# A graph attention layer: picking rows out of SBUF from the first step to the last, parts of x made in the start-up, and a reordered end

## The chip, the cores and the metric

The kernel runs on one core of one Trainium2 chip. The metric is the device time of one execution in microseconds; before the change it is 1790.13 us, the median of 3 runs (1790.07 to 1792.62).

## The reference, cut to what matters

There are 6250 nodes with 64 features and 206250 edges, sorted by destination. Queries, keys and values are linear in x; every edge weighs them with a projection of its own attributes.

```python
Qh = (x @ Wq.T + bq).reshape(n, H, D)          # H = 4, D = 16
Kh = (x @ Wk.T + bk).reshape(n, H, D)
Vh = (x @ Wv.T + bv).reshape(n, H, D)
Ee = (edge_attr @ We.T + be).reshape(-1, H, D)
score = (Kh[src] * Qh[dst] * (1.0 / np.sqrt(D)) * Ee).sum(-1)
score = jnp.exp(jnp.clip(score, -5.0, 5.0))
msg = Vh[src] * score[..., None]
wV = jax.ops.segment_sum(msg, dst, num_segments=n)
out = layernorm(x + wV)
```

## The kernel before, in words

**Tiles, groups, steps.** 128 edges make a tile (1612 tiles), 8 tiles a group (202 groups; the last has 4 tiles). A step is two groups (steps 0 to 96), and in the end one group (steps 97 to 104): NS is 105. In a tile an edge is a partition; a step's k and v lie in one of five buffers kvs (KVB), step s in number s % 5.

**The start-up.** Keys and values of all nodes go into the table kv_tab in DRAM (L320 to L323), queries, split into three bf16 parts, into q_tab (L350 to L360). For the first four groups (steps 0 and 1) the rows of x are gathered instead of k and v (L230, xs), turned on TensorE (L375, tp), copied (L378, xe), and multiplied with the weights (L380 adds the bias, L382), and the result is copied to kvs (L384). There are eight such halves, one after another. Then GpSimd gathers k and v for steps 2 and 3 (L402, one indirect DMA a tile), and the main branch begins.

**A step.** `products` (L602, L603) multiplies k by the queries and the edge projection, `scores` (L609 to L612) sums, clips and exponentiates, `message` (L619, L622) multiplies v by the score. The message is split into three bf16 parts by `minus` (L630 takes away what L632 has copied, twice), and `sums` of the next step (L638) adds the edges of each destination with one-hot matrices (L585, of), `add` (L652) puts that into accumulators. The queries of the next step come from a window of the query table by one-hot rows (`spread` L555, `onehot_rows` L572 and L577, `queries` L595). `edges` (L388, L391) projects the edge attributes. PSUM tiles of queries and edge projections have one buffer each, so a step's queries come after the last remainder of the step before.

**Where k and v of a tile come from.** Most tiles are gathered by GpSimd (`gather`, called with s + 4 in step s, behind the message). For every sixth step one tile is fetched row by row from SP's queue (`fetch_rows`, `rows_fetched`). And for steps 6 to 96 the last two tiles are *picked*: x is kept in SBUF as three bf16 parts (parts, 50 blocks of 125 rows), and a one-hot matrix of the source (hot, 25 blocks a half, made on DVE from the turned sources, L481) picks the rows by 50 matrix products (L491) for each tile. `sources` (L466, far, on ACT) and `sources_turned` (L471) give the sources, `picked` (L498, xp) adds the three parts, `picked_turned` (L505, L507) turns them, `picked_kv` (L513 to L516) makes k and v. Step s picks for step s + 2. Constants: M0 = 4 is the first picking step, LAST = 94 the last.

**The parts.** They are made in steps 0 to 3 (`table_parts`, `table_parts_rest`): x comes in again on SP's queue (raw, L448), ACT and DVE split it (L450 to L458). A memset clears the tile first (L427).

**Order.** The schedule is written out by hand: each engine executes its instructions in the order of the program, and each waits for its operands by semaphores. The order of a step is the loop that the change edits (L708 to L786).

**The end.** Blocks of 128 destinations are closed as they fill up (`close`, L668), their statistics taken (`spreads`, L677 and L678), and normed in batches (`roots` L681 and L682, `scales` L685, `norm` L688, with a DMA out, L691). The last block is added from PSUM by `last_add` (L696, L697).

Of the kernel before, what the change touches and what calls it, by code (L numbers as in the profile page):

```python
# [14 lines left out]
P = 128  # L15
N = 6250
# [21 lines left out]
CB = 10  # L38
KVB = 5
XG = 4  # L40
TB = 8
M0 = 4
PAD = N
SPARE = N + 1
TABLES = 4
# [12 lines left out]
def groups_of(s):  # L58
    return range(STEPS[s][0], STEPS[s][0] + STEPS[s][1])
# [1 line left out]

LAST = NS - 8 - 3


def picks_in(s):
    return M0 <= s <= LAST

# [33 lines left out]
def tile_gnn(ctx: ExitStack, tc: tile.TileContext, x, xT, wT, bias, beT, weT, eT, src, dst, dst_rows,  # L103
# [50 lines left out]
    be_p = consts.tile([3, G, C], BF16, name="be_p")  # L154
    wkv = consts.tile([P, 2, 2 * C], F32, name="wkv")
    bkv_p = consts.tile([3, G // 2, 2 * C], BF16, name="bkv_p")
    minus_b = consts.tile([P, P], BF16, name="minus_b")

    acc = consts.tile([P, RING, 4, C], F32, name="acc")
# [24 lines left out]
    with tc.tile_pool(name="nodes", bufs=1) as nodes, \  # L184
# [182 lines left out]
            fetch_queries(g)  # L367


        for g in range(XG):  # L370
            for h in range(2):
                tp = npsum.tile([P, 2, P], F32, name="tp", bufs=2)
                for u in range(2):
                    j = 4 * h + 2 * u
                    nc.tensor.transpose(tp[:, u, :],  # L375
                                        XS[g][:, j:j + 2, :].rearrange("p j c -> p (j c)"), ident)
                xe = nodes.tile([P, 2, P], F32, name="xe", bufs=2)
                nc.scalar.activation(xe, tp, AF.Copy)  # L378
                pv = npsum.tile([P, 4, 2 * C], F32, name="pv", bufs=2)
                nc.tensor.matmul(pv, ones_b, bkv_p, start=True, stop=False, skip_group_check=True)  # L380
                for u in range(2):
                    nc.tensor.matmul(pv[:, 2 * u:2 * u + 2, :], xe[:, u, :], wkv, start=False,  # L382
                                     stop=u == 1, skip_group_check=True)
                nc.scalar.activation(kv_of(g)[:, 4 * h:4 * h + 4, :], pv, AF.Copy)  # L384

    def edge_values(pe, et, n):

# [6 lines left out]
    def keys(t0):  # L394

        n = min(KEYS, T - t0)
        nc.vector.tensor_scalar(key_i[:, :n], dst_i[:, t0:t0 + n], P - 1, None, op0=OP.bitwise_and)
        nc.vector.tensor_copy(key[:, t0:t0 + n], key_i[:, :n, None].to_broadcast([P, n, 2]))

    def gather_kv(g, j):  # L400
        t = g * G + j
        nc.gpsimd.indirect_dma_start(  # L402
            out=kv_of(g)[:, j, :], out_offset=None, in_=kv_tab[:, :],
            in_offset=bass.IndirectOffsetOnAxis(ap=src_i[:, t:t + 1], axis=0))

    for g in range(XG, 2 * KVB - 2):
        for j in range(G):
            gather_kv(g, j)

    rv = nc.values_load(n_wide[0:1, 0:1], min_val=0, max_val=NR2 * 4)  # L410

    with tc.If(rv == 0) as branch:

        with tc.tile_pool(name="work", bufs=2) as work, \
# [11 lines left out]
            parts = accp.tile([P, NB, 3, C], BF16, name="parts")  # L426
            nc.vector.memset(parts, 0.0)  # L427
            NX = N // NB
            x_v = x.rearrange("(p b) c -> p b c", p=NX)
            n_picks = LAST - M0 + 1  # L430
            src_f = accp.tile([P, n_picks, 2], F32, name="src_f")
            t0 = (M0 + 3) * 2 * G - 2
            for i in range(2):
                nc.vector.tensor_copy(src_f[:, :, i],
                                      src_i[:, t0 + i:t0 + i + 2 * G * (n_picks - 1) + 1:2 * G])
            pick = fixed.tile([P, 4 * P], F32, name="pick")
            rows3 = pick[:, :6 * C].rearrange("p (k i c) -> p k i c", k=2, i=3)
            HOT, FAR, X = {}, {}, {}
# [2 lines left out]

                return ap.rearrange("p (a b) -> p a b", b=2)

            def table_parts(b):

                n = min(TB, NB - b)
                raw = work.tile([P, TB, C], F32, name="raw", bufs=1)
                nc.sync.dma_start(raw[:NX, :n], x_v[:, b:b + n, :])  # L448
                rest = pick[:NX, :n * C].rearrange("p (b c) -> p b c", b=n)
                nc.scalar.activation(rest, raw[:NX, :n], AF.Copy)  # L450
                nc.scalar.activation(parts[:NX, b:b + n, 0], raw[:NX, :n], AF.Copy)
                return rest

            def table_parts_rest(b, rest):
                n = min(TB, NB - b)
                nc.vector.tensor_sub(rest, rest, parts[:NX, b:b + n, 0])
                nc.scalar.activation(parts[:NX, b:b + n, 1], rest, AF.Copy)
                nc.vector.tensor_sub(parts[:NX, b:b + n, 2], rest, parts[:NX, b:b + n, 1])  # L458

            def sources(s, i):  # L460

                if picks_in(s):
                    FAR[s, i] = work.tile([P, P], BF16, name="far")
                    nc.scalar.activation(FAR[s, i], row50, AF.Identity,  # L466
                                         bias=src_f[:, s - M0, i:i + 1], scale=-1.0)
# [42 lines left out]
            def picked_kv(s):  # L510
                if picks_in(s):
                    xe, kv = X.pop(s)
                    nc.tensor.matmul(kv, ones_b, bkv_p[:, :2], start=True, stop=False,  # L513
                                     skip_group_check=True)
                    nc.tensor.matmul(kv, xe, wkv, start=False, stop=True, skip_group_check=True)  # L515
                    nc.scalar.activation(kvs[(s + 2) % KVB][:, 2 * G - 2:, :], kv, AF.Copy)  # L516

            def gather(s):
                for g in groups_of(s):
                    for j in range(tiles_of(g)):  # L520
                        if is_rowed(s) and (g - STEPS[s][0]) * G + j == COLUMN:
                            continue
                        if not picks_in(s - 2) or g == STEPS[s][0] or j < G - 2:
                            gather_kv(g, j)

            RS, RK = {}, {}
# [157 lines left out]
            def scales(lo, hi):  # L684
                nc.vector.reciprocal(rstd[:, lo:hi], rstd[:, lo:hi])  # L685
# [12 lines left out]
                                               op0=OP.mult, op1=OP.add)  # L698

            closed, scaled, normed = 0, 0, 0  # L700
            keys(0)
            for k, g in enumerate(groups_of(0)):
                onehot_rows(g, spread(g))
# [1 line left out]
                edges(0, k)  # L705
            queries(0)
            onehot_edges(0)
            for s in range(NS):  # L708
                more = s + 1 < NS
                for g in groups_of(s):  # L710
# [9 lines left out]
                    onehot_rows_rest(nexts[0])  # L720
                if s:
                    sums(s - 1)
                sources_turned(s, 1)
                sources_turned(s + 1, 0)
                if nexts[1:]:
                    onehot_rows(nexts[1], spread(nexts[1]))
                making = [b for b in range(s * 2 * TB, (s + 1) * 2 * TB, TB) if b < NB]
                if making:
                    rest = table_parts(making[0])
                prod = products(s)  # L730
                picked(s - 1)
                if more:
                    edges(s + 1, 0)
                picks(s, 0, 0)
# [5 lines left out]
                msg = message(s, score)  # L740
                if s + KVB - 1 < NS:
                    gather(s + KVB - 1)
                picked_turned(s - 1)
                if nexts[1:]:
                    edges(s + 1, 1)
                minus(s, msg, 0)
                hots(s, 1, 0)
                picks(s, 0, 1)
                minus(s, msg, 1)
                picked_kv(s - 1)  # L750
                if not more:

                    close(B - 2)
                    spreads(B - 2)
                hots(s, 1, 1)
                picks(s, 1, 0)
                sources(s + 1, 1)
                sources(s + 2, 0)
                if s + 1 < NS:
                    rows_fetched(s + 1)  # L760
                if more:
# [1 line left out]
                        keys(nexts[0] * G)  # L763
                    onehot_edges(s + 1)
                    queries(s + 1)
                picks(s, 1, 1)
                hots(s + 1, 0, 0)
                hots(s + 1, 0, 1)
                if more:
# [13 lines left out]
                for i, b in enumerate(making):  # L783
                    if i:
                        rest = table_parts(b)
                    table_parts_rest(b, rest)  # L786
# [12 lines left out]
    with branch.Else():  # L799

        sums = [dram.tile([NR, C], F32, name=f"sums{i}") for i in range(TABLES)]
        with tc.tile_pool(name="gconsts", bufs=1) as gc, \
                tc.tile_pool(name="gloads", bufs=3) as loads, \
                tc.tile_pool(name="ggath", bufs=4) as gath, \
# [28 lines left out]
            def gather(g, j):  # L833
                if j == 0:
                    Q[g] = gath.tile([P, G, C], F32, name="gq")
                t = g * G + j
                if g >= 2 * KVB - 2:
# [125 lines left out]
```

## Time and profile before

| what | number |
|---|---|
| the profiled execution | 1789.88 us, span 1788.0 us |
| mean granted TensorE clock | 0.951 |
| PE | 1638.5 us busy, 92% of the span, 15751 instructions |
| DVE | 1481.6 us, 83% |
| ACT | 914.0 us, 51% |
| POOL | 1337.4 us, 75% |
| gathers of k and v (L402) | 1383, mean 944 ns |
| rows fetched on SP's queue (rk) | 1920 |
| picks (L491) | 9100 matrix products, 828.3 us |
| hots (L481) | 364, mean 1813 ns |

The page gives for each engine its busy time, then groups of equal instructions with their number, mean time and the idle time in front of them. POOL is GpSimd; SP issues most DMAs; PEld is TensorE's loading of weights, which overlaps its products. A timeline line has start and length in us, engine, line of the program, operation, output and inputs with their shapes, how many, and in brackets how long the engine had been idle and what ended that.

### The profile page before, as it was taken

To read this page: it belongs to the slowest core of one execution; us is meant where nothing else is said; L and a number is where in the kernel's file an instruction comes from. 1 tells how busy PE (TensorE), PEld (TensorE's weight loads), DVE (VectorE), ACT (ScalarE), POOL (GpSimd) and SP (SyncE) were. 2 spreads that over 40 slices of the span, in tenths; PEclk is the share of its full clock that TensorE was granted. 3 is DMA by queue.
4 is the path that set the end of the run, shared out by engine and by line. 5 is a ranking of instruction groups with operands and counts; after the bars stand their busy time and mean duration, and the time that the engine had idled before them with its cause. 6 is when DMAs were issued, how large, how long until landed. Compare 5 with 4: busy or idle time off the path is not lost.

```text
span 1788.0 us, 44286 instructions
## 1 busy us (share of the span) xinstructions
PE 1638.5 (92%) x15751; PEld 1369.6 (77%) x15751; DVE 1481.6 (83%) x1695; ACT 914.0 (51%) x1328; POOL 1337.4 (75%) x1427
## 2 busy tenths in 40 slices
PE   8978999999999998999999899999989998999864
PEld 8647888888888787787887778777877887787632
DVE  6459999999998898888889888888988888898654
ACT  3465555555554464454455445455544554455443
POOL 7777777777777777777777777777777777777774
PEclk9968999999999999999999999999999999999855
DMA  7443333333333333332333333323332333333331
GB/s 221 132 121 84 90 93 94 93 94 92 93 81 94 93 86 89 92 94 80 93 93 81 93 81 93 92 81 99 87 93 80 94 93 81 93 90 81 91 80 44
DMA packets 109970, 166.71 MB, mean 93 GB/s; under 512 B 69196, under 2 KB 71452, under 8 KB 109626
## 3 DMA queue, kind: packets, MB, share of 16 engines
q0 software_dynamic: 45280, 91.78, 19.4%
q1 hardware_dynamic: 64074, 71.01, 14.1%
q8 instruction: 125, 2.05, 0.5%
q10 hardware_dynamic: 384, 1.00, 0.3%
q14 instruction: 107, 0.88, 0.2%
HBM read 156.33 MB, written 7.33 MB: 92 GB/s over the span
## 4 chain that ended last, share of the span: by engine, by line
PE 38%; POOL 29%; issue 14%; DVE 13%; DMA 4%; ACT 3%; DVEq 0%; SPq 0%; POOLq 0%; ACTq 0%
POOL kv L402 29%; PE pick L491 18%; PE pe L391 5%; DVE hot L481 5%; DMA kv<-kv_tab,src_i 3%; PE pq L630 2%; PE small L638 2%; DVE prod L603 2%; DVE prod L602 2%; PE pb L555 2%; PE pe L388 2%; PE pb L515 1%; PE pq L595 1%; DVE pq L619 1%; PE ps L350 1%
## 5 line engine op out<-in xcount | busy, mean ns | idle before, releaser
L402 POOL DMA_INDIRECT kv<-kv_tab,src_i x1383 | 1305.3, 944 | 421.7 <-issue 399.8
L491 PE MATMUL pick<-parts,hot 128*128 128x192 bf16 x9100 | 828.3, 249 | 0.0
L491 PEld LDWEIGHTS <-hot 128*128 128x128 bf16 x9100 | 771.7, 99 | 38.1
L481 DVE TENSOR_TENSOR hot<-small,block 128x3200 bf16<-128x3200 bf16 x364 | 645.3, 1813 | 0.4 <-PE pick L491 0.4
L572 ACT ACTIVATE to<-pb,minus_row 126x1024 bf16<-126x1024 f32 x202 | 222.7, 1102 | 371.0 <-PE pb L555 367.2
L632 ACT ACTIVATE msg<-pq 128x1024 bf16<-128x1024 f32 (+2 forms) x210 | 207.6, 989 | 222.3 <-PE pq L630 222.3
L391 PEld LDWEIGHTS pe<-we_sb,et 128*128 128x128 f32 x1612 | 209.7, 203 | 133.4 <-issue 95.3
L602 DVE TENSOR_TENSOR prod<-kv,pq 128x1024 f32<-128x1024 f32 (+2 forms) x105 | 123.5, 1176 | 169.3 <-DMA kv<-kv_tab,src_i 52.0
L391 PE MATMUL pe<-we_sb,et 128*128 128x128 f32 x1612 | 250.3, 302 | 0.0
L577 ACT ACTIVATE to<-to,one_p 126x1024 bf16<-126x1024 bf16 x202 | 230.6, 1142 | 3.5
L638 PEld LDWEIGHTS <-of 128*128 128x128 bf16 x1612 | 145.3, 102 | 31.1 <-issue 7.9
L638 PE MATMUL small<-msg,of 128*128 128x192 bf16 x1612 | 161.9, 257 | 0.5 <-ACT msg L632 0.5
L388 PE MATMUL pe<-be_p,ones_b 3*128 3x512 bf16 x202 | 79.7, 395 | 86.3 <-DVE prod L603 86.1
L630 PE MATMUL pq<-msg,minus_b 128*128 128x512 bf16 x404 | 128.0, 396 | 33.1 <-ACT msg L622 19.5
L622 ACT ACTIVATE msg<-pq 128x1024 bf16<-128x1024 f32 (+2 forms) x105 | 103.8, 989 | 96.8 <-DVE pq L619 96.8
L609 DVE TENSOR_REDUCE small<-prod 128x64 f32<-128x1024 f32 (+2 forms) x105 | 123.6, 1177 | 14.5 <-PE small L471 8.8
L555 PE MATMUL pb<-key_rows,ident_b 112*128 112x512 bf16 x403 | 127.9, 400 | 2.8 <-ACT to L572 2.8
L603 DVE TENSOR_TENSOR prod<-prod,pe 128x1024 f32<-128x1024 f32 (+2 forms) x105 | 123.6, 1177 | 3.6
L619 DVE TENSOR_TENSOR pq<-kv,small 128x1024 f32<-128x1024 f32 (+2 forms) x105 | 123.4, 1175 | 1.4 <-ACT small L612 1.4
L585 DVE TENSOR_TENSOR of<-small,key 128x2048 bf16<-128x2048 bf16 (+2 forms) x105 | 122.9, 1171 | 0.3
L595 PEld LDWEIGHTS <-to 126*128 126x128 bf16 x1612 | 63.5, 101 | 25.3 <-issue 25.1
L612 ACT ACTIVATE small<-small 128x64 f32<-128x64 f32 (+2 forms) x105 | 21.7, 207 | 111.1 <-DVE small L611 109.2
(129 smaller groups left out, 996.4 us busy)
## 6 DMA issues: line engine op xcount, KB each, us to landing
et<-in_eT SPq DMA_DIRECT2D x100, 512.0 KB
rk<-kv_tab SPq DMA_DIRECT2D x1920, 0.5 KB
kv<-kv_tab,src_i POOLq DMA_INDIRECT x1383
qw<-q_tab SPq DMA_DIRECT2D x202, 15.8 KB
kv_tab<-kv_sb SPq DMA_DIRECT2D x5, 640.0 KB
q_tab<-q SPq DMA_DIRECT2D x5, 480.0 KB
acc<-in_x SPq DMA_DIRECT2D x48, 32.0 KB
out<-y SPq DMA_DIRECT2D x48, 32.0 KB
```

The lines of the kernel that those rows point to most:

```text
L391: nc.tensor.matmul(pe[:, 2 * u:2 * u + 2, :], et[:, u, :], we_sb, start=False, stop=u == n // 2 - 1, skip_group_check=True)
L402: nc.gpsimd.indirect_dma_start(out=kv_of(g)[:, j, :], out_offset=None, in_=kv_tab[:, :], in_offset=bass.IndirectOffsetOnAxis(ap=src_i[:, t ...
L481: nc.vector.tensor_tensor(HOT[s, i, h].rearrange("p b (a c) -> p b a c", c=2), pairs(from_b[i])[:, None].to_broadcast(shape), block2[:, bl ...
L491: nc.tensor.matmul(rows3[:, i], hot[:, k, :], parts[:, b], start=b == 0, stop=b == NB - 1)
L555: nc.tensor.matmul(pb[:, b:b + 4, :], ident_b[:NR2, g // 2:g // 2 + 1].to_broadcast([NR2, P]), key_rows[:, g % 2, b * P:(b + 4) * P], star ...
L572: nc.scalar.activation(TO[g][:, :n, :], pb[:3 * W, :n, :], AF.Square, bias=minus_row3[:3 * W])
L577: nc.scalar.activation(TO[g][:, :n, :], TO[g][:, :n, :], AF.Relu, bias=one_p[:3 * W], scale=-1.0)
L602: nc.vector.tensor_mul(prod[:, :n, :], kvs[s % KVB][:, :n, :C], PQ[s][:, :n, :])
L603: nc.vector.tensor_mul(prod[:, :n, :], prod[:, :n, :], PE[s][:, :n, :])
L630: nc.tensor.matmul(msg[:, lo:hi, :], minus_b, M3[s][:, lo:hi, i, :], start=False, stop=True, skip_group_check=True)
L632: nc.scalar.activation(M3[s][:, :n, i + 1, :], msg[:, :n, :], AF.Copy)
L638: nc.tensor.matmul(PA[s], OH[s][:, j, :], M3[s][:, j], start=j == 0, stop=j == n - 1)
```

## The change

It does four things.

- Picking runs from step 0 to the last steps. Steps 0 to 96 pick two tiles for step s + 2; after that three pairs are picked over two single steps each (97 and 98 for step 100, 99 and 100 for 102, 101 and 102 for 104). `second_of` says whose second tile a step works on. 18 gathers less are issued: two in each of steps 2, 3, 4, 5, 97, 98, 100, 102 and 104. The program has 1365 gathers of k and v in this branch, 10050 picks and 402 hots.
- The parts of x are made in the start-up, from xT_sb, which is in SBUF there anyway: four blocks of 128 rows at a time are turned on TensorE into a ps tile, split by ACT and DVE. Thirteen such blocks stand between the k and v of the first groups, two to a half, and the next half's rows are turned ahead of them. The memset and the loads of raw go; parts moves into the pool of constants.
- Before step 0 the first sources, and the hots of its first tile, are made.
- At the end `last_add`, `spreads` and `roots` of the last block go ahead of `scales` and `norm` of the block before it.

The other branch (not executed with these inputs) loses one buffer and gathers what the first loop no longer does.

```diff
-TB = 8
-M0 = 4
+TB = 4
-LAST = NS - 8 - 3
+LAST = NS - 8 - 1
+PAIRS = [*range(LAST + 1), *range(LAST + 1, NS - 3, 2)]
+TARGET = {p: p + (2 if p <= LAST else 3) for p in PAIRS}
-def picks_in(s):
-    return M0 <= s <= LAST
+def picks_in(p):
+    return p in PAIRS
+def second_of(s):
+    return s if s <= LAST else s - 1 if s - 1 in PAIRS else None
+def is_picked(g, j):
+    s = max(s for s in range(NS) if STEPS[s][0] <= g)
+    return s in TARGET.values() and g == groups_of(s)[-1] and j >= tiles_of(g) - 2
...
+        def x_turned(g, h):
+            tp = npsum.tile([P, 2, P], F32, name="tp", bufs=2)
+            for u in range(2):
+                j = 4 * h + 2 * u
+                nc.tensor.transpose(tp[:, u, :], XS[g][:, j:j + 2, :].rearrange("p j c -> p (j c)"),
+                                    ident)
+            xe = nodes.tile([P, 2, P], F32, name="xe", bufs=2)
+            nc.scalar.activation(xe, tp, AF.Copy)
+            return xe
...
+        def parts_of_x(b):
+            n = min(TB, NB - b)
+            px = npsum.tile([P, 2, 2 * C], F32, name="ps").rearrange("p i (j c) -> p (i j) c", j=2)
+            px = px[:, :n]
+            for u in range(n):
+                nc.tensor.transpose(px[:, u, :], xT_sb[:C, (b + u) * P:(b + u + 1) * P],
+                                    ident[:C, :C])
+            nc.scalar.activation(parts[:, b:b + n, 0], px, AF.Copy)
+            nc.vector.tensor_sub(px, px, parts[:, b:b + n, 0])
+            halves.append((px, b, n))
+        def rest_of_x():
+            px, b, n = halves.pop(0)
+            nc.scalar.activation(parts[:, b:b + n, 1], px, AF.Copy)
+            nc.vector.tensor_sub(parts[:, b:b + n, 2], px, parts[:, b:b + n, 1])
+        xe = x_turned(*order[0])
+        for i, gh in enumerate(order):
+            following = x_turned(*order[i + 1]) if i + 1 < len(order) else None
+            for b in blocks[2 * i:2 * i + 2]:
+                parts_of_x(b)
+            first_kv(*gh, xe)
+            xe = following
+            while halves:
+                rest_of_x()
...
     for g in range(XG, 2 * KVB - 2):
         for j in range(G):
-            gather_kv(g, j)
+            if not is_picked(g, j):
+                gather_kv(g, j)
...
+            sources(0, 0)
+            sources_turned(0, 0)
             keys(0)
...
             onehot_edges(0)
+            sources(0, 1)
+            sources(1, 0)
+            for h in range(2):
+                hots(0, 0, h)
             for s in range(NS):
...
-                sources_turned(s, 1)
+                sources_turned(second_of(s), 1)
                 sources_turned(s + 1, 0)
...
-                making = [b for b in range(s * 2 * TB, (s + 1) * 2 * TB, TB) if b < NB]
-                if making:
-                    rest = table_parts(making[0])
                 prod = products(s)
-                picked(s - 1)
+                picked(second_of(s - 1))
...
-                picked_turned(s - 1)
+                picked_turned(second_of(s - 1))
...
-                hots(s, 1, 0)
+                hots(second_of(s), 1, 0)
                 picks(s, 0, 1)
                 minus(s, msg, 1)
-                picked_kv(s - 1)
+                picked_kv(second_of(s - 1))
...
-                hots(s, 1, 1)
-                picks(s, 1, 0)
-                sources(s + 1, 1)
+                hots(second_of(s), 1, 1)
+                picks(second_of(s), 1, 0)
+                sources(second_of(s + 1), 1)
                 sources(s + 2, 0)
...
-                picks(s, 1, 1)
+                picks(second_of(s), 1, 1)
                 hots(s + 1, 0, 0)
                 hots(s + 1, 0, 1)
...
             close(B - 1)
-            scales(B - 2, B - 1)
-            norm(B - 2)
             last_add(NS - 1)
             spreads(B - 1)
             roots(B - 1, B)
+            scales(B - 2, B - 1)
+            norm(B - 2)
             scales(B - 1, B)
             norm(B - 1)
```

More of the change, by code (lines that the diff above doesn't have):

```diff
@@ L156, in tile_gnn @@
     bkv_p = consts.tile([3, G // 2, 2 * C], BF16, name="bkv_p")
+    parts = consts.tile([P, NB, 3, C], BF16, name="parts")
     minus_b = consts.tile([P, P], BF16, name="minus_b")
@@ L367, in tile_gnn @@
             fetch_queries(g)
[L370 to L384, printed above, removed]
+        def x_turned(g, h):
[7 more added lines that the diff above has]
+            return xe
@@ new lines, in first_kv @@
+        def first_kv(g, h, xe):
+            pv = npsum.tile([P, 4, 2 * C], F32, name="pv", bufs=2)
+            nc.tensor.matmul(pv, ones_b, bkv_p, start=True, stop=False, skip_group_check=True)
+            for u in range(2):
+                nc.tensor.matmul(pv[:, 2 * u:2 * u + 2, :], xe[:, u, :], wkv, start=False,
+                                 stop=u == 1, skip_group_check=True)
+            nc.scalar.activation(kv_of(g)[:, 4 * h:4 * h + 4, :], pv, AF.Copy)
+        halves = []
+        def parts_of_x(b):
[8 more added lines that the diff above has]
+            halves.append((px, b, n))
@@ new lines, in rest_of_x @@
+        def rest_of_x():
+            px, b, n = halves.pop(0)
+            nc.scalar.activation(parts[:, b:b + n, 1], px, AF.Copy)
+            nc.vector.tensor_sub(parts[:, b:b + n, 2], px, parts[:, b:b + n, 1])
+        order = [(g, h) for g in range(XG) for h in range(2)]
+        blocks = list(range(0, NB, TB))
+        xe = x_turned(*order[0])
[7 more added lines that the diff above has]
+                rest_of_x()
@@ L424, in tile_gnn @@
             nc.tensor.transpose(col, row_b[:, 0:1].to_broadcast([P, P]), ident_b)
[L426 to L432, printed above, removed]
-            for i in range(2):
-                nc.vector.tensor_copy(src_f[:, :, i],
-                                      src_i[:, t0 + i:t0 + i + 2 * G * (n_picks - 1) + 1:2 * G])
+            src_f = accp.tile([P, PAIRS[-1] + 1, 2], F32, name="src_f")
+            full = NS - 8 - 2
+            for i in range(2):
+                t0 = 3 * 2 * G - 2 + i
+                nc.vector.tensor_copy(src_f[:, :full, i],
+                                      src_i[:, t0:t0 + 2 * G * (full - 1) + 1:2 * G])
+            for p in PAIRS[full:]:
+                t0 = STEPS[TARGET[p]][0] * G + tiles_in(TARGET[p]) - 2
+                nc.vector.tensor_copy(src_f[:, p], src_i[:, t0:t0 + 2])
             pick = fixed.tile([P, 4 * P], F32, name="pick")
@@ L442, in pairs @@
                 return ap.rearrange("p (a b) -> p a b", b=2)
[L444 to L458, printed above, removed]
             def sources(s, i):
@@ L466, in sources @@
                     nc.scalar.activation(FAR[s, i], row50, AF.Identity,
-                                         bias=src_f[:, s - M0, i:i + 1], scale=-1.0)
+                                         bias=src_f[:, s, i:i + 1], scale=-1.0)
             def sources_turned(s, i):
@@ L515, in picked_kv @@
                     nc.tensor.matmul(kv, xe, wkv, start=False, stop=True, skip_group_check=True)
-                    nc.scalar.activation(kvs[(s + 2) % KVB][:, 2 * G - 2:, :], kv, AF.Copy)
+                    n = tiles_in(TARGET[s])
+                    nc.scalar.activation(kvs[TARGET[s] % KVB][:, n - 2:n, :], kv, AF.Copy)
             def gather(s):
@@ L522, in gather @@
                             continue
-                        if not picks_in(s - 2) or g == STEPS[s][0] or j < G - 2:
+                        if not is_picked(g, j):
                             gather_kv(g, j)
@@ L782, in tile_gnn @@
                             normed += 1
[L783 to L786, printed above, removed]
             assert normed == B - 2
@@ L803, in tile_gnn @@
                 tc.tile_pool(name="gloads", bufs=3) as loads, \
[L804 removed]
+                tc.tile_pool(name="ggath", bufs=3) as gath, \
                 tc.tile_pool(name="gwork", bufs=2) as work, \
@@ L836, in gather @@
                 t = g * G + j
-                if g >= 2 * KVB - 2:
+                if g >= 2 * KVB - 2 or is_picked(g, j):
                     gather_kv(g, j)
```

## The prediction, made before the changed kernel ran

> **What bounds the kernel now.** I read the costliest groups first, then the waits, the windows, and the timeline at both ends.
>
> ```profile
> L402 POOL DMA_INDIRECT kv<-kv_tab,src_i x1383 | 1305.3, 944 | 421.7 <-issue 399.8
> ...
> L481 DVE TENSOR_TENSOR hot<-small,block 128x3200 bf16<-128x3200 bf16 x364 | 645.3, 1813 | 0.4 <-PE pick L491 0.4
> ```
>
> ```profile
> POOL kv L402 <- issue: 399.8, 1311, 0.3
> ```
>
> In the second (who waited for whom: total, times, longest) the reader is to see the last number. Busy and idle of the gathers make 1727.0 us for 1383, a pitch of 1.2487 us, and no gap before one is over 0.3 us. So POOL never waits for work: it runs from the first gather (43.04 in the timeline) to 1769.79. What comes after that is a tail of 18 us.
>
> ```profile
> 180.00:225.00 45.00, 45.00 (x474) 38.84 (x475) 42.67 (x42) 23.66 (x36) 34.02 (x37) 1.00 0.33 89
> ...
> 1710.00:1755.00 45.00, 30.64 (x152) 18.71 (x150) 24.22 (x56) 23.71 (x33) 34.08 (x36) 0.58 0.32 84
> ```
>
> The columns are the stretch, its length, busy time of PE, PEld, DVE, ACT, POOL, then granted clock, DMA share, GB/s. In the first row PE and DVE are full: a step with picks needs 15.65 us of PE, while its 14 gathers need 17.5. POOL starts some 40 us ahead, loses 1.6 us a step and is the pace from about 390 us on; the last eight steps (97 to 104, one group each, no picks) are something else, the third view:
>
> ```profile
> 1746.68 0.69 DVE L602 TENSOR_TENSOR prod<-kv,pq 128x512 f32<-128x512 f32 x1 [2.59 <-PE pq L595]
> ...
> 1753.85 0.94 POOL L402 DMA_INDIRECT kv<-kv_tab,src_i  x1 [0.30 <-issue]
> 1754.08 0.58 PE L595 MATMUL pq<-qw,to 126*128 126x64 bf16 x8 [0.69 <-ACT msg L632]
> ...
> 1756.58 0.69 DVE L602 TENSOR_TENSOR prod<-kv,pq 128x512 f32<-128x512 f32 x1 [4.27 <-PE small L638]
> ...
> 1758.58 2.08 PE L391 MATMUL pe<-we_sb,et 128*128 128x128 f32 x8
> ```
>
> Step 101 starts its product at 1746.68; its queries (L595) for step 102 end at 1754.66, 8.0 us later, and the product of 102 then waits for its last gather (issue ends 1754.79, 1.8 us to land). So a single step has an 8 to 8.6 us chain of its own (product, score, message, two remainders, queries) beside 10 us of POOL. The product starts of steps 96 to 104 are 1696.65, 1708.91, 1718.43, 1728.84, 1738.05, 1746.68, 1756.58, 1766.65, 1774.05: only 102 and 103 clearly wait for gathers. From 96 to 104 it is 77.4 us, of which the gathers could give back about 3.5.
>
> **Removed gathers.** 18 of 1383 go: 8 in steps 2 to 5, 10 in steps 97, 98, 100, 102, 104. At 1.2487 that is 10.0 us ahead of step 96, and 12.5 behind it, the latter of use only if POOL still sets the pace there.
>
> **The start.** POOL's own start (43.04) isn't touched. Its first wait is for a buffer: step 5 is gathered into step 0's buffer and needs the message of step 0 (L619).
>
> ```profile
> 76.37 0.60 ACT L384 ACTIVATE kv<-pv 128x512 f32<-128x512 f32 x1 [2.16 <-PE pv L382]
> ...
> 77.08 1.06 PE L555 MATMUL pb<-key_rows,ident_b 112*128 112x512 bf16 x2
> ...
> 84.97 1.22 DVE L602 TENSOR_TENSOR prod<-kv,pq 128x1024 f32<-128x1024 f32 x1 [1.24 <-PE pq L595]
> ...
> 90.33 1.23 DVE L619 TENSOR_TENSOR pq<-kv,small 128x1024 f32<-128x1024 f32 x1 [1.36 <-ACT small L612]
> ```
>
> That message ends at 91.56 now; the gathers of step 5 begin at 102.9, 11 us of slack. After: POOL is there 6 gathers sooner for steps 2 to 4 (28+14 gathers, 43.04 + 42 x 1.2487 = 95.5). The message comes later. Fifty 64-row transposes of x stand in PE's queue among the first k and v, where PE is already full (8.00 of 8.00 in each of the windows 60 to 68 and 68 to 76). A transpose isn't in the trace in this shape; nearest is L350 (same weight load, 17.99 us for 84, 0.214 each): 10.7 us. Bounds: 0.12, the f32 weight load at full clock (L391, 0.97 for 8), 6 us; 0.43, the spacing of L375's two weight loads, 21 us. I take 10.7, less 0.7 for the wait for xe that goes (4.1 in all, mostly under L380): 10. Their 26 copies on ACT (0.38 each) and 26 subtractions on DVE (0.42) lie beside PE, with both nearly idle there; without that cover some 10 us each. Then the first turning of sources comes before L555 in PE's queue, behind src_f (DVE, 0.5 after small's first write) and far (ACT, 0.4): 1.6 us. Gone from the first steps are the memset (4.06, under the wait for L595 until 84.97: worth 0), the raw loads on SP, and L450 and L451 ahead of the exponential of step 0 (0.9). The 3.6 us of hots ahead of product 0 fill the memset's place. Message 0 then ends at 91.56 + 10 + 1.6 - 0.9 + 0.3 = 102.6, and **POOL idles 7.1 us** at its first gather of step 5 (bounds 3 and 18). The gathers of step 6 come up 14 pitches later, at 120, and their buffer (step 1's) is free at about 118: no second stall. Nothing else stands behind the waiting gather than the later gathers, and nobody needs them yet: the price is paid from about step 30 on, where POOL sets the pace. Product 96 so moves by -10.0 + 7.1 = **-2.9 us**. Steps 0 to 3 took 16 us each on the slow chain of the parts; with picks they take 15.65.
>
> **The end.** Here hots (1.81 us each, the L481 row) enter steps 96 to 102: 4, 2, 4, 0, 4, 0, 2. The diff also does one thing twice: `second_of(97)` is 96, as it is for 96, so step 97 repeats two hots and 50 picks of pair 96. In DVE's order hots stand behind the message and ahead of the next product. A single step's DVE rows in the timeline: first product 0.72 to the next start, second 0.69, score 0.69, clip 0.2, 0.5 until the exponential is back, two adds 0.66, message 0.66: it ends 4.0 after the product's start if the sums of the step before are out of the way, 4.6 with xp (0.55). Then a pair of hots 3.54, of 0.68, norms 0.76.
> - Step 96: the full step's DVE chain, 14.55 (product 1645.36 to the end of hots 1659.91), with a shorter of (-0.5) and a close (1.1): 15.1.
> - 97: PE's queue (full clock, it was just busy): edges from 1.45 to 2.95 (L388 and L391, 1.5), 25 picks (2.06) to 5.0, the turn of xp to 5.3, first remainder, 25 picks to 7.6, second remainder 8.0, k and v of the pair 8.9, 25 picks 10.95, queries 11.5: 11.6 (DVE needs 9).
> - 98: on DVE products 1.4, xp after PE's last 25 picks 2.65, then the wait for the sums queued behind those picks 3.5, message 6.05, hots 9.6, of 10.3, hots 13.8, close 14.9, root and three norms: 16.3.
> - 100: message 4.0, hots 7.6, of 8.2, hots 11.8, norms: 12.6. 102: 9.0.
> - 99 and 101: 50 picks lie between the message and the queries: 10.7 (an exp table load included) and 9.5 at full clock. 103 with xp and k and v of the pair: 8.2.
>
> Here a rule counts. The Trainium skill (TensorE: Matmul & The Clock Gate, "What's actually happening") says the array runs at half clock after about 3.4 us of idleness and doubles after as much sustained work. The rows agree: L391's eight take 2.08 at the end, where the clock is 0.58, 1.16 at 1648, and 25 picks after a wait 3.74 (at 1666) against 2.23. By the rule alone picks would warm the tail and pay for some of themselves; but 98 and 100 leave PE idle for over 3 us, so 99 and 101 begin cold: 12.1 each. I take the middle, 11.4 and 10.8. Sum: 15.1 + 11.6 + 16.3 + 11.4 + 12.6 + 10.8 + 9.0 + 8.2 = 95.0, against 77.4: **+17.6** (all warm +15.6, all cold +20.4). A clock or a hidden wait can't take it below what DVE alone has to do, 74 us in these steps by the same rows (some 42 now, 29 of hots, 3 of xp), so the lower end is -3, if nothing waited for anything; I keep to the chain. The gathers of 97 to 104 are through some 20 us earlier than used, so their 12.5 us are worth nothing.
>
> **The last norms.** In DVE's order the last sum t (L696, 1781.12) stands behind the root, scale and norm of the block before; its sums are out of PE at 1780.0. With these moved behind it, t starts about 0.8 sooner, and the two norms end close together: **-0.7** (bounds 0 and -1). The pool of 3 buffers instead of 4 lies in the branch that isn't run: 0.
>
> **Sum.** Profiled execution: 1789.88, span 1788.0, 1.9 around it. -2.9 + 17.6 - 0.7 = +14.0: span 1802.0, time 1803.9; the median of the runs is 0.25 above the profiled one: **1804**.
>
> **Rivals.**
> 1. POOL still paces the tail (faster). The hots would fit in DVE's idle time: it is busy 24.2 of 45 us in 1710 to 1755. Then all 22.5 us count, less 7.1 and 0.7 more: 1774. It decides if the picking steps average under 8.6 us. Against it: DVE's queue is in order, 29 us of added hots are bunched, four in one step, and idle DVE time is mostly waiting on the chain.
> 2. No stall at step 5 (transposes at 0.12, buffer free by 96): 1790.1 - 10.0 + 17.6 - 0.7 = 1797, slower still.
> 3. Start and tail worse: transposes at 0.43 (stall 18) and a cold tail: 1818.
> 4. A wash: no stall, warm tail, and a repeated pair that hides (3 us): 1792.
>
> **Chances.** Main case 0.68, own range 1798 to 1811 (the stall from 3, tail +15.6 to +20.4 and one us either way). Rival 1: 0.09; 2: 0.09; 3: 0.09; 4: 0.05. Main, 2 and 3 are slower. About 0.2% (3.6 us) is what a measurement can tell from no change: faster 0.09, same 0.05, slower 0.86. Range for 8 in 10: 1792 to 1814 (rivals 1 and 3 stay outside).
>
> **What would show it.** Right: one gap of some 7 us on POOL near 95 and none after; product 96 about 3 us earlier; POOL's last gather near 1754, with 20 us of slack; DVE full in steps 98 and 100, those 16 and 13 us long; 10050 picks. Wrong: POOL's gap absent (2), product waits on gathers in 97 to 103 and steps of 8 to 10 us (1), transposes of x at over 0.3 us each (3).

## The result, and the profile after

The changed kernel takes 1799.1 us, the median of 5 runs (1797.59 to 1802.61), against 1790.13 before (5 runs, 1790.07 to 1792.62): a ratio of 1.0049, with a 95% interval of 1.0034 to 1.0064. It is half a per cent slower. The profiled execution took 1800.04 us with a span of 1798.2, so 10.2 us of span more than before. Eleven of the twelve experiments below ran on three chips on which the kernel before itself takes 3066 to 3100 us, and one (the end's order) on a chip on which it takes 1792; so the total times of the eleven tell nothing about the 1799, and from their traces only stretches are read that the disturbance leaves alone.

The page's groups, with the same columns as before:

```profile
L448 POOL DMA_INDIRECT kv<-kv_tab,src_i x1365 | 1288.7, 944 | 417.9 <-issue 395.7
L521 PE MATMUL pick<-parts,hot 128*128 128x192 bf16 x10050 | 914.7, 249 | 0.0
...
L511 DVE TENSOR_TENSOR hot<-small,block 128x3200 bf16<-128x3200 bf16 x402 | 712.5, 1813 | 0.1
```

18 gathers are gone, and 38 hots came (67.2 us of DVE). Who waited for whom, for the gathers:

```profile
POOL kv L448 <- issue: 395.7, 1298, 0.3
...
POOL kv L448 <- DVE pq L650: 2.4, 2, 2.1
```

The second line is new: POOL waited twice for a message (L650), once for 2.1 us. The timeline at that place, with the message of step 0 and the first gather of step 5:

```profile
94.70 0.94 POOL L448 DMA_INDIRECT kv<-kv_tab,src_i  x1 [0.30 <-issue]
96.23 1.23 DVE L650 TENSOR_TENSOR pq<-kv,small 128x1024 f32<-128x1024 f32 x1 [0.27 <-ACT small L643]
...
97.73 0.94 POOL L448 DMA_INDIRECT kv<-kv_tab,src_i  x1 [2.08 <-DVE pq L650]
```

2.08 where 0.30 is usual: a stall of 1.8 us. No other gap ahead of a gather is over 0.35. The windows of the prediction:

```profile
180.00:225.00 45.00, 44.77 (x470) 38.37 (x471) 41.88 (x46) 24.76 (x36) 33.95 (x36) 1.00 0.35 93
1710.00:1755.00 45.00, 36.35 (x347) 30.42 (x346) 34.16 (x49) 19.85 (x34) 30.18 (x32) 0.92 0.28 75
```

The middle is as it was. In the tail DVE does 34.16 us of work where it did 24.22, and TensorE's granted clock is 0.92 where it was 0.58. Steps 96 and 97, from product to product, before:

```profile
1696.65:1708.91 12.26, 5.46 (x31) 3.07 (x30) 7.28 (x11) 4.42 (x5) 9.21 (x11) 0.64 0.21 54
1708.91:1718.43 9.52, 6.26 (x38) 4.03 (x37) 4.21 (x8) 4.23 (x6) 7.39 (x8) 0.68 0.42 115
```

and after:

```profile
1689.09:1704.75 15.66, 14.39 (x156) 12.70 (x154) 14.68 (x17) 6.27 (x9) 11.93 (x13) 1.00 0.21 56
1704.75:1716.57 11.82, 11.82 (x130) 10.53 (x128) 8.13 (x12) 5.41 (x10) 8.85 (x10) 1.00 0.36 98
```

Step 96 is now filled by DVE (14.68 of 15.66 us), step 97 by PE (all of 11.82). What DVE does in step 98, product to product:

```profile
1716.57 0.69 DVE L633 TENSOR_TENSOR prod<-kv,pq 128x512 f32<-128x512 f32 x1 [2.63 <-issue]
...
1718.57 0.56 DVE L528 TENSOR_REDUCE xp<-pick 128x128 f32<-128x384 f32 x1 [0.60 <-PE pick L521]
...
1722.08 0.69 DVE L650 TENSOR_TENSOR pq<-kv,small 128x512 f32<-128x512 f32 x1
1722.67 3.55 DVE L511 TENSOR_TENSOR hot<-small,block 128x3200 bf16<-128x3200 bf16 x2
...
1726.74 3.54 DVE L511 TENSOR_TENSOR hot<-small,block 128x3200 bf16<-128x3200 bf16 x2
...
1729.19 0.40 PE L626 MATMUL pq<-qw,to 126*128 126x64 bf16 x8
...
1732.71 0.68 DVE L633 TENSOR_TENSOR prod<-kv,pq 128x512 f32<-128x512 f32 x1
```

The queries (L626) are there at 1729.6, but the next product starts at 1732.71, because four hots, a close, a root and three norms stand ahead of it in DVE's queue.

From the starts of the products the whole difference can be added up (us):

| stretch | before | predicted | after | after, end's order restored |
|---|---|---|---|---|
| start of product 96 | 1696.65 | 1693.8 | 1689.09 | 1689.63 |
| step 96 | 12.26 | 15.1 | 15.66 | 15.25 |
| 97 | 9.52 | 11.6 | 11.82 | 11.81 |
| 98 | 10.41 | 16.3 | 16.14 | 16.16 |
| 99 | 9.21 | 11.4 | 10.26 | 10.26 |
| 100 | 8.63 | 12.6 | 12.50 | 12.51 |
| 101 | 9.90 | 10.8 | 8.99 | 8.98 |
| 102 | 10.07 | 9.0 | 11.40 | 10.46 |
| 103 | 7.40 | 8.2 | 9.53 | 9.66 |
| product 104 to the end | 13.95 | 13.25 | 12.81 | 13.98 |

Product 96 is 7.6 us earlier, the eight steps take 96.3 instead of 77.4 (18.9 more), the end 1.1 less: -7.6 + 18.9 - 1.1 = +10.2. POOL's last gather ends at 1749.62, 35.8 us ahead of product 104; before it was 4.3. Product 96 still starts 1.9 us after the last of its gathers, as before the change, but the gathers of steps 97 to 103 end 10.1 to 28.7 us ahead of their products, where it was 1.8 to 4.2: from step 97 on POOL is no longer waited for.

### The profile page after: what moved, and what is told of

The parts are those of the page before. It is cut to its first block, busy times and chain, and to the rows that moved or that the text cites. A ratio compares the mean times of both kernels' runs of the same rounds, so it can differ in the third digit from the quotient of the medians.

```text
span 1798.2 us, 46506 instructions
## 1 busy us (share of the span) xinstructions
PE 1694.6 (94%) x16810; PEld 1439.7 (80%) x16810; DVE 1548.2 (86%) x1759; ACT 920.4 (51%) x1372; POOL 1321.1 (73%) x1409
## 5 line engine op out<-in xcount | busy, mean ns | idle before, releaser
L448 POOL DMA_INDIRECT kv<-kv_tab,src_i x1365 | 1288.7, 944 | 417.9 <-issue 395.7
L521 PE MATMUL pick<-parts,hot 128*128 128x192 bf16 x10050 | 914.7, 249 | 0.0
L521 PEld LDWEIGHTS <-hot 128*128 128x128 bf16 x10050 | 852.0, 99 | 46.1 <-issue 2.2
L511 DVE TENSOR_TENSOR hot<-small,block 128x3200 bf16<-128x3200 bf16 x402 | 712.5, 1813 | 0.1
L437 PEld LDWEIGHTS pe<-we_sb,et 128*128 128x128 f32 x1612 | 200.5, 195 | 113.6 <-issue 73.8
L437 PE MATMUL pe<-we_sb,et 128*128 128x128 f32 x1612 | 239.9, 293 | 0.0
L669 PEld LDWEIGHTS <-of 128*128 128x128 bf16 x1612 | 136.6, 98 | 26.1 <-issue 1.5
L669 PE MATMUL small<-msg,of 128*128 128x192 bf16 x1612 | 151.2, 247 | 0.5 <-ACT msg L663 0.5
L661 PE MATMUL pq<-msg,minus_b 128*128 128x512 bf16 x404 | 122.2, 381 | 18.9 <-ACT msg L653 14.2
L650 DVE TENSOR_TENSOR pq<-kv,small 128x1024 f32<-128x1024 f32 (+2 forms) x105 | 123.4, 1175 | 0.3 <-ACT small L643 0.3
L586 PE MATMUL pb<-key_rows,ident_b 112*128 112x512 bf16 x403 | 121.7, 383 | 1.5 <-ACT to L603 1.0
L683 DVE SCALAR_TENSOR_TENSOR acc<-small,above,acc 128x192 f32<-128x192 f32 x103 | 43.0, 417 | 39.3 <-ACT small L643 37.9
L545 PE MATMUL pb<-wkv,xe 128*128 128x256 f32 x202 | 71.6, 437 | 0.0
```

The lines of the kernel that those rows point to most:

```text
L437: nc.tensor.matmul(pe[:, 2 * u:2 * u + 2, :], et[:, u, :], we_sb, start=False, stop=u == n // 2 - 1, skip_group_check=True)
L448: nc.gpsimd.indirect_dma_start(out=kv_of(g)[:, j, :], out_offset=None, in_=kv_tab[:, :], in_offset=bass.IndirectOffsetOnAxis(ap=src_i[:, t ...
L511: nc.vector.tensor_tensor(HOT[s, i, h].rearrange("p b (a c) -> p b a c", c=2), pairs(from_b[i])[:, None].to_broadcast(shape), block2[:, bl ...
L521: nc.tensor.matmul(rows3[:, i], hot[:, k, :], parts[:, b], start=b == 0, stop=b == NB - 1)
L650: nc.vector.tensor_mul(msg[:, :n, :].rearrange("p g (h d) -> p g h d", h=H), kvs[s % KVB][:, :n, C:].rearrange("p g (h d) -> p g h d", h=H ...
L669: nc.tensor.matmul(PA[s], OH[s][:, j, :], M3[s][:, j], start=j == 0, stop=j == n - 1)
```

## The experiments

The theory: the picks of the tail lengthen steps 96 to 103, since hots stand in DVE's queue ahead of the next product and picks in PE's ahead of the queries, while the gathers that they replace weren't what these steps waited for. The rivals: the loss lies in the start-up or in the end's order; POOL still sets the pace of the tail; PE's picks alone, or DVE's hots alone, are the cost.

On the three chips with the long times TensorE often stands still, most of all while POOL gathers (last section). In their traces nothing is gathered in steps 100 to 103 (one gather at the start of step 100 at most), and there the traces agree: step 100 of a kernel with these picks takes 12.50 us in the changed kernel's and 12.51 in that with the end's order restored, and 12.49, 12.49, 12.50, 12.50 and 12.19 on the three chips. So these four steps of the tail's eight are read; steps 96 to 99 are not.

**No picks for the tail, or fewer.** One line (picks_to_96 also leaves out the repeated pair, by the line of no_repeat below):

```diff
-PAIRS = [*range(LAST + 1), *range(LAST + 1, NS - 3, 2)]
+PAIRS = [*range(LAST - 1)]     # no_tail_picks, pairs 0 to 94
+PAIRS = [*range(LAST)]         # picks_to_95_now
+PAIRS = [*range(LAST + 1)]     # picks_to_96
```

> Pairs 0 to 94 alone are picked, so steps 97 to 104 are gathered as before the change; start-up, first picks and end order stay as changed. Theory (the picks of the tail lengthen steps 96 to 103 by 18.9 us, and the first picks are worth 7.6 us): product 96 at 1689 as in the changed kernel, 77.4 us from product 96 to product 104 as before, time about 1781, faster than both. Rival (the loss sits in the start-up or in the new order, the tail only shows it): the tail stays near 96 us and the time near 1799. Second rival (the gathers of the tail are worth something, so gathering them again costs POOL 10 x 1.2487 us): the tail comes back longer than 77.4 and the time is 1785 to 1793.

> Pairs 0 to 94 alone are picked, so steps 97 to 104 are gathered as before the change; start-up, first picks and end order stay as changed. Theory: product 96 at 1689 as in the changed kernel, 77.4 us from product 96 to product 104 as before (36 us of it in steps 100 to 103, two of which wait for gathers), 12.8 after it, time about 1781, faster than both. Rival (the loss sits in the start-up or in the new order): time near 1799.

> Pairs 0 to 95 are picked (pair 95 is for step 97, and its picks and hots lie in step 95, where POOL sets the pace), none after. Two gathers less than with pairs to 94. Theory: step 96 gets no hots and stays near 12.3, the waits for gathers in steps 102 and 103 (3.6 us by the chain without waits) shrink by up to 2.5, time 1778 to 1781, the fastest. Rival (any pick for a single step costs more than its gather): above the version with pairs to 94.

> Pairs 0 to 96 (targets 2 to 98), none for single steps from 99 on, no repetition. Four gathers less than with pairs to 94; two hots more in step 95, four in step 96. Theory: step 96 stays near 15, the rest of the tail is that of the gathers, with 5 us less of them: product 96 to 104 is 77 to 80, time 1780 to 1784. Rival (any hots in the tail cost their whole time): 6 hots, 10.9 us more than without, about 1792.

Totals against the kernel before on the same chip: 3093.69 (ratio 1.0076, 1.0062 to 1.0089), 3113.37 (1.0071, 1.0058 to 1.0085), 3119.08 (1.0090, 1.0076 to 1.0103), 3122.88 (1.0094, 1.0079 to 1.0109). None of the forecasts of a total (1778 to 1784) could be tested there. The steps 100 to 103, by windows (length, busy PE, PEld, DVE, ACT, POOL, granted clock), in the changed kernel:

```profile
1742.97:1755.47 12.50, 9.57 (x83) 7.86 (x83) 11.71 (x15) 4.68 (x8) 5.13 (x6) 0.86 0.14 36
1755.47:1764.46 8.99, 8.17 (x82) 6.79 (x81) 5.24 (x14) 4.93 (x9) 0.00 (x0) 1.00 0.12 26
1764.46:1775.86 11.40, 8.41 (x57) 6.48 (x57) 8.33 (x13) 4.39 (x7) 0.00 (x0) 0.70 0.04 10
1775.86:1785.39 9.53, 6.83 (x52) 4.86 (x51) 4.17 (x8) 3.94 (x8) 0.00 (x0) 0.86 0.00 0
```

and with pairs 0 to 94 alone (the first of the two runs):

```profile
3053.25:3061.34 8.09, 5.81 (x30) 3.74 (x29) 4.87 (x11) 4.23 (x6) 0.94 (x1) 0.71 0.12 29
3061.34:3069.90 8.56, 6.43 (x30) 3.82 (x29) 4.87 (x11) 4.24 (x6) 0.00 (x0) 0.50 0.07 15
3069.90:3078.46 8.56, 6.42 (x30) 3.82 (x29) 4.88 (x11) 4.24 (x6) 0.00 (x0) 0.50 0.06 13
3078.46:3085.64 7.18, 4.24 (x22) 2.67 (x21) 3.61 (x7) 3.38 (x6) 0.00 (x0) 0.74 0.00 0
```

Without picks the four steps take 32.4 us (33.3 in the second run, 33.3 and 32.6 with pairs to 95 and 96), with picks 42.4 in the changed kernel and 41.3 to 42.6 in the six other traces that have them whole. On each of the three chips the two kinds lie 9 to 10 us apart. DVE is full in step 100 (11.71 of 12.50); without the hots it is idle for some 40% of it. In the traces without picks the gathers end 31 us and more ahead of the products of steps 100 to 104, so 32.4 to 33.3 is the bare chain; the kernel before, on its own chip, took 36.0 with its gathers. The picks so cost some 9 to 10 us here and save 2.7 to 3.6 us of waiting for gathers, an estimate across chips. That start-up and end's order are as changed in these kernels, while the steps are short, leaves the picks as the cause of the longer steps 100 to 103. From product 96 to product 104 it is 85.5 us without them and 104.5 with them on one chip, 86.2 and 106.8 on another: 19.1 and 20.5 apart, near the 18.9 above, but steps 96 to 99 are in it, which are disturbed there.

**Hots alone, picks alone**, for the pairs of the tail:

```diff
 # tail_hots_alone, in picks()
                     hot = HOT.pop((s, i, h))
+                    if s > NS - 11:
+                        return
 # tail_picks_alone, in hots(); still is a tile of zeros, made once
+                    if s > NS - 11:
+                        HOT[s, i, h] = still
+                        return
```

> For pairs 95 on (targets 97 to 104) the hots are made but the 50 matrix products a tile that pick with them are left out, so those tiles get wrong k and v. Theory (DVE's order costs most: the hots stand behind the message and ahead of the next product; but in steps 97, 99, 101 the picks lie between message and queries): steps 98 and 100 stay near 16 and 12, steps 96, 97, 99, 101 fall by 1 to 2.5 us each, product 96 to 104 about 88 us, time about 1791. Rival (the picks on PE are the cost): tail near 78, time about 1781.

> For pairs 95 on the picks are done with a tile of zeros that is made once, and the hots are left out, so those tiles get wrong k and v. Theory: steps 98 and 100 fall to about 10 us each, product 96 to 104 about 84 us, time about 1787. Rival (picks on PE are the cost): tail stays near 95, time about 1798. Hots and picks overlap in part, so the two savings need not add up to 18.9.

The forecasts from product 96 to 104 (88 and 84 us) have the disturbed steps in them and couldn't be tested. Totals 3118.5 (1.0081, 1.0066 to 1.0096) and 3135.43 (1.0133, 1.0115 to 1.0150). Steps 100 to 103 of the hots alone, then of the picks alone:

```profile
3064.35:3077.52 13.17, 6.94 (x37) 4.02 (x37) 11.71 (x15) 6.98 (x10) 0.00 (x0) 0.63 0.00 1
3077.52:3086.42 8.90, 6.86 (x30) 4.05 (x29) 5.26 (x13) 2.62 (x7) 0.00 (x0) 0.50 0.14 28
3086.42:3096.03 9.61, 6.94 (x35) 4.41 (x35) 8.25 (x13) 5.17 (x9) 0.00 (x0) 0.68 0.00 0
3096.03:3104.54 8.51, 5.77 (x24) 3.28 (x23) 3.99 (x10) 3.19 (x7) 0.00 (x0) 0.50 0.05 12
```

```profile
3075.37:3085.80 10.43, 7.49 (x59) 5.98 (x59) 4.88 (x12) 4.68 (x8) 0.00 (x0) 0.84 0.06 13
3085.80:3096.69 10.89, 10.43 (x108) 8.85 (x106) 5.44 (x13) 4.72 (x9) 0.00 (x0) 1.00 0.05 11
3096.69:3106.80 10.11, 7.12 (x58) 5.46 (x58) 4.88 (x11) 4.39 (x7) 0.00 (x0) 0.83 0.05 11
3106.80:3115.42 8.62, 5.92 (x55) 4.49 (x53) 4.18 (x9) 3.94 (x8) 0.00 (x0) 1.00 0.00 0
```

The sums are 40.2 and 40.1, each 6.8 to 7.8 us over the bare chain, and the two together add only 1 to 2.5 more. So neither rival of one engine holds: leave out either, and most of the cost stays. The hots make step 100 long (13.17), the picks steps 101 and 102 (10.89, 10.11). A part is common to both, the sources, xp, its turn and k and v: step 103, with neither hots nor picks, still takes 8.51 instead of 7.2 to 7.6. Step 100 came out as I expected with the picks alone (10.43 for 10), but was longer than the 12 expected with the hots alone: there its score waits 1.09 us for the turned sources, and TensorE's clock is 0.63, with the picks 0.73 or 0.86. The two kernels are no clean halves, since without the picks TensorE is at 0.50 to 0.68 in these steps, and with them alone at 0.83 to 1.00.

**Tail gathered as well as picked.**

```diff
-    return s in TARGET.values() and g == groups_of(s)[-1] and j >= tiles_of(g) - 2
+    return s < NS - 8 and s in TARGET.values() and g == groups_of(s)[-1] and j >= tiles_of(g) - 2
```

> Tiles picked for steps 97 to 104 are also gathered (10 gathers more, behind step 96), the picks stay. Theory (POOL runs 25 to 36 us ahead in the tail, so the gathers taken away there are worth nothing): time within 1 us of the changed kernel, 1799. Rival (POOL still sets the pace in the tail): up to 12.5 us more, 1811.

Total 3126.73 (1.0186, 1.0166 to 1.0206). Steps 100 to 103 take 41.3, not more than without the ten gathers, but all gathers were over by then. The total is 11.0 above that of the kernel with the transposes twice on the same chip, which has the same picks; but 8.2 of it lies in steps 96 to 99 (70.1 against 61.9), which are disturbed on this chip. The run decides little, for here POOL is 42 to 93 us ahead of the products of the tail in any case. That the ten gathers were worth nothing rests on the leads in the changed kernel's own trace: they would take 2.5 us of the 10.1 by product 97 and 12.5 of the 35.8 by product 104.

**Early picks, repeated pair, transposes twice.**

```diff
-PAIRS = [*range(LAST + 1), *range(LAST + 1, NS - 3, 2)]
+PAIRS = [*range(4, LAST + 1), *range(LAST + 1, NS - 3, 2)]     # no_early_picks (and one index to match)
-    return s if s <= LAST else s - 1 if s - 1 in PAIRS else None
+    return s if s <= LAST else s - 1 if s - 1 in PAIRS and s - 1 > LAST else None   # no_repeat
-            for u in range(n):
+            for u in [*range(n), *range(n)]:      # parts_turned_twice, twice run
```

> Picks start at pair 4 as before the change; parts of x still made in the start-up, picks of the tail and end order as changed. Theory: 8 gathers come back ahead of step 96, POOL has no gap longer than 0.3 us, product 96 is back at about 1696.6 and the time is about 1807. Rival (making the parts in the start-up costs the start more than the first picks save): time at or under 1799.

> Step 97 no longer repeats the second half of pair 96 (2 hots, 50 picks, one xp, one turn, one k and v less: 10000 picks, 400 hots). Theory: step 97 falls from 11.8 to about 9.3, step 98 by about 1, time about 3.5 us less, 1795.6. Rival (the repetition hides beside the chain): within 1 us of 1799.

> Each of the 50 transposes of x for the parts is issued twice, same result. Theory (message 0 frees the buffer that POOL's first gather of step 5 waits for, and what POOL loses there is never made up): message 0 later by 50 x 0.139 = 6.9 us, POOL's gap from 2.1 to about 9 us, time about 1806. Rival (a delay in the start is absorbed by step 96): gap longer, time still near 1799.

> Each of the 50 transposes of x for the parts is issued twice, same result. Theory (what POOL loses while its first gather of step 5 waits for message 0 is never made up): the 6.25 halves get 0.86 us longer each, message 0 later by 5.4 us, POOL's gap from 2.1 to about 7.5 us, product 96 later by as much, time about 1804.5. Rival (a delay in the start is absorbed by step 96): gap longer, time still near 1799.

Totals: 3089.12 (1.0059, 1.0046 to 1.0073), 3132.36 (1.0126, 1.0110 to 1.0142), 3115.72 (1.0145, 1.0125 to 1.0166) and 3136.78 (1.0145, 1.0129 to 1.0160). The first two settle nothing: what the first picks save, and whether the repetition hides, lies in steps that gather. That a late message 0 costs its whole delay wasn't settled either. The start-up did answer one question. The changed kernel's transposes in two halves that follow one another:

```profile
60.50 1.11 PE L409 MATMUL ps<-ident,xT_sb 64*128 64x64 f32 x8
...
64.51 1.11 PE L409 MATMUL ps<-ident,xT_sb 64*128 64x64 f32 x8
```

and with each of them twice:

```profile
115.79 1.97 PE L409 MATMUL ps<-ident,xT_sb 64*128 64x64 f32 x16
120.66 1.97 PE L409 MATMUL ps<-ident,xT_sb 64*128 64x64 f32 x16
```

A half goes from 4.01 to 4.87 us, 0.86 for eight transposes more: 0.107 each, so some 5.4 us for all 50. (On the chip of the second pair of rows a half without the doubling takes 4.01 too.) Against the kernel before, where a half takes 3.04 us, the first eight cost 0.97, or 0.12 each.

**The end's order restored.**

```diff
             close(B - 1)
+            scales(B - 2, B - 1)
+            norm(B - 2)
             last_add(NS - 1)
             spreads(B - 1)
             roots(B - 1, B)
-            scales(B - 2, B - 1)
-            norm(B - 2)
```

> The end's order is that of before (scale and norm of the block before the last ahead of the last sum), all else as changed. Theory: from product 104 to the end of the span 13.9 us instead of 12.8, so 1.1 us more time. Rival (the order is worth nothing, since the last DMA of the output sets the end): 12.8 as with the change.

On the chip where before takes 1792.25 this took 1800.49 (1.0049, 1.0026 to 1.0072). From product 104 to the end it is 13.98 us, against 12.81 and 13.95: the order is worth 1.1 to 1.2. In the span it doesn't show, since steps 96 to 103 are 1.2 us shorter here, 0.9 of it in step 102 (TensorE's clock, below). With the old order the last sum (L727) waits for the norm:

```profile
1784.72 0.42 DVE L633 TENSOR_TENSOR prod<-kv,pq 128x256 f32<-128x256 f32 x1 [4.14 <-ACT kv L547]
...
1791.37 0.31 DVE L719 TENSOR_SCALAR y<-y,stats,rstd 128x64 f32<-128x64 f32 x1
1791.60 0.35 DVE L727 TENSOR_REDUCE t<-small 128x64 f32<-128x192 f32 x1
```

With the new order it waits only for the sums:

```profile
1791.18 0.36 DVE L727 TENSOR_REDUCE t<-small 128x64 f32<-128x192 f32 x1 [1.34 <-PE small L669]
```

It starts 6.88 us after product 104 with the old order, in the changed kernel 5.79. The run is also a second look at the rest of the change: the step lengths repeat within 0.1 us in 97 to 101, and POOL has no stall at all (its longest wait is 0.35). Product 96 is none the earlier for that (1689.63), because the gathers are a little slower on this chip: from the 43rd to the 1301st it takes 1572.9 us, in the changed kernel's trace 1571.1.

## Why the prediction was right, and where it wasn't

The direction, the place and the mechanism held; 1804 was 4.9 us too much. By its own steps:

- **Removed gathers, -10.0.** The number and the pitch are as said: 1365 gathers, one every 1.249 us outside the stall.
- **The stall, +7.1.** This is the term that was mis-sized: 1.8 us, and none in the second trace of the same start-up. The waiting gather and the buffer were right. Message 0 ends at 97.46 (95.35 in the other trace) instead of the 102.6 I had, 5.9 and 3.8 us later than before rather than 11. The error is the transposes' price, 0.214 each from a row of f32 products with the same weights, 10 us in all; a transpose takes 0.139 by its row and costs 0.107 to 0.12 in the queue, and the last copy of the first k and v ends 82.74 instead of 76.97, 5.8 later. The lower bound, 0.12 from a weight load, was the near one. The sources' turn ahead of L586 cost 1.15 (1.6 said). Product 96 moved by -7.6, not by -2.9: 4.7 us of the miss. (-10.0 and +1.8 make -8.2; POOL's first gather starts 0.3 later, and the other 0.3 is not accounted for.) What a microsecond of stall costs at step 96 was not isolated by a run.
- **The tail, +17.6.** It is +18.9. Steps 96, 97, 98 and 100 lie within 0.6 of the forecast. 99 and 101 are 1.1 and 1.8 shorter, since I had put half a cold start into them, and TensorE was at full clock again before they began: 1.00 in both, where the chain without picks has 0.50 in 101. 102 and 103 are 2.4 and 1.3 longer. So the sum is near by some luck: -2.9 in two steps and +3.7 in two others, with +0.5 in the other four. In 102 the 25 picks that wait for the hots run cold, 4.20 us instead of 2.23, and hold back the queries:

```profile
1768.77 3.54 DVE L511 TENSOR_TENSOR hot<-small,block 128x3200 bf16<-128x3200 bf16 x2
...
1771.19 4.20 PE L521 MATMUL pick<-parts,hot 128*128 128x192 bf16 x25
...
1775.19 0.63 PE L626 MATMUL pq<-qw,to 126*128 126x64 bf16 x8
```

In 103 the pair's last 25 picks go ahead of the sums, and the score starts 3.0 us after the product, where it was 1.5 before; k and v of the pair then go ahead of the queries.
- **The clock.** In every trace here the granted clock is 1.00 or 0.50, and it changes only at points whose distances are multiples of 3.41 us. In the changed kernel's tail it is 0.50 from 1724.67 to 1728.07 (step 98), from 1748.55 to 1751.97 (100) and from 1769.03 to 1775.87 (102). Three such stretches in step 98:

```profile
1721.27:1724.67 3.40, 0.54 (x2) 0.10 (x1) 3.25 (x5) 1.48 (x5) 2.78 (x3) 1.00 0.23 58
1724.68:1728.06 3.38, 3.38 (x16) 2.47 (x16) 3.38 (x3) 2.16 (x3) 2.49 (x3) 0.50 0.21 56
1728.08:1731.49 3.41, 3.41 (x48) 3.41 (x47) 3.28 (x6) 0.08 (x1) 2.50 (x4) 1.00 0.17 46
```

One in which PE does little (0.54 of 3.40) is followed by one at half the clock, and once PE has been busy for all of that one the clock is full. The prediction's step that failed for 99 and 101 is this: it let PE idle for over 3 us in 98 and 100, so that they would begin cold. PE's longest gap there is 2.2 us; the clock did fall, but inside 98 and 100, and it was full again when 99 and 101 began. The Trainium skill (TensorE: Matmul & The Clock Gate, "What's actually happening") adds that the window which decides runs free, so that the same kernel can warm up at different points. The traces agree: with the same instructions step 100 has one stretch at half clock or two (0.86 or 0.73 on average), and step 101 then takes 9.0 or 9.9 to 10.1 us (82 to 84 against 96 to 98 products of PE in it); step 102 had two or one (0.70 or 0.84) and took 11.4 or 10.5. A single value for such a step is good to about 1 us; the sum of the four moved by 1.3.
- **The last norms, -0.7.** -1.1.
- **Sum.** +14.0 was said and +10.2 came: -4.7 from the stall, +1.3 from the tail, -0.4 from the end. The remaining 1.1 of the 4.9 is that the median of the runs lies 0.9 under the profiled one, where 0.25 above it was forecast.
- **The rivals.** "POOL still paces the tail" is out: it needed steps under 8.6 us and they average 12.0. "No stall", 1797, was nearer than my main case; the profiled run lies between the two. The transposes at 0.43 and the wash are out.
- **Readings and sums that were off, without effect on the forecast.** The product of step 101 too starts 1.9 us after its last gather, not only those of 102 and 103. Of steps 0 to 3 before the change, three took 16 us and step 3 took 12.9. The tail "all cold" is +19.6 by its own figures, not +20.4. By its own figures too POOL's last gather (1754) would have been some 35 us ahead of its product (product 96 at 1693.8, and 95.0 behind it), not 20; it was 35.8.

What the experiments don't show: the cost of the picks in steps 96 to 99 (12.5 of the 18.9 us) rests on the traces with 1790 to 1800 us, where no kernel without these picks was run, and on the reading of steps 96 to 98; what the first picks save by themselves and the price of the repeated pair are open, and so is whether the kernel with pairs to 94 or 95 beats both on a chip where before takes 1790. The sum above (product 96 at 1689, the old tail of 77.4, the new end) would make it 1781, but that is only argued.

## What to carry to other kernels

Before work is moved from the engine that paces to others, ask stage by stage whether it paces there: here eight gathers taken away ahead of step 96 are worth 1.25 us each, less what the start then loses (7.6 of 10.0 us arrived), and ten in the last steps at most 3.6 us together, while the replacement stands in an in-order queue between a message and the next product: the four hots of step 98, 7.1 us of DVE, made it 5.7 us longer. A cost on two engines isn't found by relieving one of them; test each alone and both. Price a new instruction by a row of the same kind: transposes at little more than half the price of a product with the same weights turned a stall of 7 us into one of 2.

## What the runs showed of the hardware

I had not expected that the same kernel takes 1792 us on one chip and 3066 to 3100 on three others. On those POOL waits for messages instead of being the pace (pairs 0 to 94):

```profile
POOL kv L448 <- DVE pq L650: 1273.0, 98, 22.6
...
PEld L626 <- issue: 767.5, 561, 5.2
PE pq L626 <- issue: 612.9, 487, 5.0
```

and TensorE stands for nothing that the profile shows, twice as often while POOL gathers as otherwise: of the time from 200 to 2900 us POOL gathers for 1519, and of PE's 847 us of such idling 609 fall into that. Two windows of one step, ahead of the gathers and during them:

```profile
1500.13:1510.33 10.20, 10.20 (x83) 8.51 (x81) 6.60 (x9) 4.83 (x7) 0.00 (x0) 0.79 0.03 6
1510.33:1528.50 18.17, 8.54 (x73) 6.33 (x72) 7.88 (x5) 3.96 (x7) 13.19 (x14) 0.81 0.26 80
```

83 products in 10.2 us, then 73 in 18.2; and single queries (L626) come out 0.7 to 1.4 us apart:

```profile
1525.94 0.27 PE L626 MATMUL pq<-qw,to 126*128 126x64 bf16 x2 [0.69 <-issue]
...
1528.07 0.21 PE L626 MATMUL pq<-qw,to 126*128 126x64 bf16 x1 [1.19 <-issue]
```

The gathers themselves keep their 0.94 us. On one of these chips, over the kernel before, 400 picks more came with 21.7 us, 500 with 27.4, and 950 (and the second set of transposes) with 45.1; the start-up and the end differ from the kernel before as well, so these aren't prices of the picks. What holds the instructions back there is open; no run was made on it.
